# A relational graph convolution on one core: sums by chunk in place of sums by four chunks, evictions on VectorE, and two tiles in five chunks copied by SyncE and ScalarE

## The chip, the core and the metric

The kernel runs on one core of a Trainium2 chip. A core has five engines, each with an instruction queue of its own that it works off in order: TensorE (PE, matmuls, with its weight loads shown as PEld), VectorE (DVE), ScalarE (ACT), GpSimd (POOL) and SyncE (SP, which here only issues DMAs). Engines wait for each other, and for DMAs, by semaphores. The metric is the device time of one execution in microseconds; smaller is better.

## The reference

Two layers of a relational graph convolution on 50,000 nodes of 128 features, 850,000 edges of which 50,000 are loops (the last of each node's run), 16 relations made of 8 bases, then a residual layer norm:

```python
def _rgcn_layer(h, src, dst, rel, basis, w_comp, loop_w, bias):
    W = jnp.einsum('rb,bio->rio', w_comp, basis)
    seg = dst.astype(jnp.int32) * N_REL + rel.astype(jnp.int32)
    agg = jax.ops.segment_sum(h[src], seg, num_segments=N_ENT * N_REL)
    agg = agg.reshape(N_ENT, N_REL, -1)
    msg = jnp.einsum('nri,rio->no', agg, W)
    out = msg + h @ loop_w + bias
    return jax.nn.relu(out)
...
h = _rgcn_layer(entity_emb, src, dst, rel_type, basis1, w_comp1, loop_w1, bias1)
h = _rgcn_layer(h, src, dst, rel_type, basis2, w_comp2, loop_w2, bias2)
return h
...
x = _layernorm(x + _L0_gnn_ref(x, ...), axis=-1)
```

The edges come sorted by their destination `dst`. All is fp32.

## The kernel before

**Tiles and chunks.** A tile is 128 edges, a chunk `K` = 10 tiles. The edges that aren't loops make `C` = 625 chunks a layer, 1,250 in both. As the edges are sorted, a tile reaches few destination nodes: each tile has a window of `WN` = 12 consecutive nodes, called slots, and a chunk 120 slots. Nodes are worked on in groups of 512 (97 or 98 a layer), each held as 128 partitions of `J` = 4 nodes.

**A chunk's way through the engines.**

- GpSimd fetches the source rows of every tile by one indirect DMA of 128 rows of 512 B (`gather`, line 202). `rows` is a ring of `GATHERS` = 5 chunks, 50 tiles; the fetch is issued `FETCH` = 2 chunks ahead in the program, and a tile's buffer may be refilled once the product of the tile that was in it (50 tiles back) is done.
- VectorE makes, per chunk, the mask of slots `own` (line 869) and the scaled mask `hot` (line 876): for each edge, basis and slot, the edge's weight in that basis where the edge belongs to that slot. The weights come from one-hot relations (`weights`, load at line 617, comparison at 624, matmuls into `fixed` at 629), once for four chunks.
- TensorE multiplies a tile's rows by its part of `hot` (line 974): 128 features by 8 bases x 12 slots. Five such products fill one PSUM bank (`pa`, two banks).
- ScalarE copies five products at a time into `aT` (line 982). `aT` holds four chunks (`BATCH` = 4), 480 slots for each basis.
- Once in four chunks `slots_of_batch` sums over the bases: eight matmuls of 480 columns with the basis as stationary operand (line 746), spread over the following tiles; ScalarE copies the result, which has the slots along its columns, into `by_slot` (line 752); TensorE turns it back with four transposes (line 756); VectorE spreads each slot's row to its place among the `J` nodes of a partition (`spread_out`, line 734, tile `slots`).
- `LAG` = 6 chunks later `to_nodes` adds the slots to the node groups in PSUM (line 788, tile `pn`, with the mask of line 771), and the loop term with `loop_w` (line 798).
- Beside that, `from_itself` works out per group of 512 nodes what the loop edges give: load `h_own` (line 677, SyncE), transposes (687), a copy to `hT` by ScalarE (691), 16 matmuls into `po` (702, two banks), each scaled by VectorE into `by` (709), and a reduction by VectorE (717). `loop_weights` gives the scales (load at 644, comparison 655, matmuls 662, copy 670).
- `finish` adds both parts (809), and does the relu (812, ScalarE) and the store to `H` (813, SyncE) in layer 0, or the residual and the layer norm (`normed`, 576 to 587) and the store to the output (818) in layer 1.

**Order.** TensorE, GpSimd, VectorE and ScalarE run in the order in which the program is written (`manual_schedule`); the function `beside` places the side work at fixed tiles of a chunk: a step of `from_itself` at tiles 0, 5 and 7, a step of the batch's sums at tiles 1, 3, 6 and 9, a step of `finish` at 2, 6 and 9, the node sums at 8. SyncE issues its loads and stores in program order too. The last five chunks of a layer are summed one by one, in `slots` (line 724): eight matmuls of 128 columns with a basis of `aT` as the stationary operand, whose result needs no transpose. An fp32 matmul shows as two records in the trace, a transpose as one.

**Set-up.** At the beginning and beside the first chunks, `runs` removes the loops from runs of 672 edges and `rows_of` puts the remaining edges' sources, slots and relations into tables (`src`, `key`, `REL`), a block of 128 rows of 640 edges at a time.

Of the kernel before, what the change touches and what calls it, by code (L numbers as in the profile page):

```python
# [40 lines left out]
I32 = mybir.dt.int32  # L41
# [31 lines left out]
BATCH = 4  # L73
LAG = BATCH + 2
# [8 lines left out]
def tile_rgcn_resnorm(  # L83
# [33 lines left out]
    assert D == P and N >= P and edges.shape[0] == 1 and AT * NR == P and PER * NB * WN <= BANK and AT * PER * NB == WEIGHTS and PER == HALF and S <= P and C >= 4 and M > 0 and N % C == 0 and N % J == 0 and J * D == BANK and C % BATCH == 1 and C > 4 * BATCH and RUN - LK // 2 == LIVE and 2 * C <= NG * P and N <= 1 << 16 and E % ROW == 0  # L117
# [9 lines left out]
    REL = dram.tile([2 * C, LIVE], U8, name="REL")  # L127
    NL = -(-(N + LK) // GN) * GN
# [309 lines left out]
    def rows_of(j, pool):  # L438
# [35 lines left out]

        begin = pool.tile([P, HALF], F32, name="begin")
# [113 lines left out]
    def chunked():  # L589
        with (  # L590
# [7 lines left out]

            ALONE = C - BATCH - 1

# [12 lines left out]
            def weights(c, n):  # L613
# [9 lines left out]
                is_rel = hp.tile([P, LIVE], F32, name="is_rel", bufs=1)  # L623
# [14 lines left out]
            def loop_weights(g, n):  # L638
# [14 lines left out]
                is_rel = rel.bitcast(F32)  # L653
                for h in range(2):
                    nc.vector.tensor_scalar(is_rel[:m, h, :], rel[:m, h, :], its_rel1[:m], None, op0=OP.is_equal)
                    if h == 0:
                        yield
                po = ps_o.tile([P, BANK], F32, name="po")
                of = po[:, : J * T * NB].rearrange("p (j t) -> p j t", j=J)
                for j in range(J):  # L660
                    for h in range(2):
                        nc.tensor.matmul(  # L662
                            of[:, j, :],
                            is_rel[:m, h, :].rearrange("k (p j) -> k p j", j=J)[:, :, j],
                            EACH[n][:m, :T, :].rearrange("k t b -> k (t b)"),
                            start=h == 0,
                            stop=h == 1,
                        )
# [4 lines left out]
            def from_itself(g, of, n):  # L673

                m = nodes(g)
                h = sb.tile([P, J, D], F32, name="h_own", bufs=1)
# [43 lines left out]
            def slots(c, k, aT, n):  # L720
# [7 lines left out]
                yield spread_out(c, ps[:, :D])  # L728

            def spread_out(c, of):  # L730

                k = ks(c) * WN
                st = sb.tile([P, J, D], F32, name="slots", bufs=BATCH)
                nc.vector.tensor_tensor(  # L734
                    st[:k],
                    of[:k, None, :].to_broadcast([k, J, D]),
                    which[:k, c, :, None].to_broadcast([k, J, D]),
                    op=OP.mult,
                )
                return st  # L740

            def slots_of_batch(c, aT, st, n):

                ps = ps_s.tile([P, BANK], F32, name="ps")
                for b in range(NB):
                    nc.tensor.matmul(  # L746
                        ps[:, : BATCH * S], BASIS[n][:, b, :], aT[:, b, :], start=b == 0, stop=b == NB - 1
                    )
                    if b < NB - 1:
                        yield  # L750
                by_slot = sb.tile([P, BATCH * S], F32, name="by_slot", bufs=1)
                nc.scalar.copy(by_slot, ps[:, : BATCH * S])  # L752
                yield
                po = ps_o.tile([P, BANK], F32, name="po")
                for q in range(BATCH):
                    nc.tensor.transpose(po[:S, q * P : (q + 1) * P], by_slot[:, q * S : (q + 1) * S], ident)  # L756
                    if q == 1:
                        yield
                for q in range(BATCH):
                    st[c + q] = spread_out(c + q, po[:, q * P : (q + 1) * P])  # L760
                    if q == 1:
                        yield
                yield
# [60 lines left out]

            loaded, stored = [0], [1]
# [36 lines left out]
            for n, of in enumerate((x, H1)):  # L862
# [21 lines left out]
                def sum_up(c):  # L884
                    at = c % BATCH * S
                    for st[c] in slots(c, ks(c), aTs[c // BATCH][:, :, at : at + S], n):
                        yield

                def added_in(c):

                    if c < ALONE + 2:
                        return [c - LAG] if c >= LAG else []
                    at = ALONE - BATCH + 2 * (c - ALONE - 2)
                    return [at, at + 1] if c < C else list(range(at, C))

                def own_of_all():

                    for g in range(NGR):
                        while now[0] < min(first(g) + LAG - 5, C - LAG - 2):
# [9 lines left out]
                def add(c):  # L909

                    for g in to_nodes(c, n):
                        assert made[0] > g
                        ending.append(finish(g, n))

                def beside(t, c, owning, summing):
# [3 lines left out]
                    if c < ALONE + 2:  # L919
                        if t in (1, 3, 6, 9):  # L920
                            next(summing, None)
                    elif 1 <= t <= 4:
                        for _ in range(NB // 4):
                            next(summing, None)
                        if t == 4:
                            done(summing)
                            if c == C - 1:
                                done(sum_up(c - 1))
# [3 lines left out]
                    if t == 8:  # L932
                        for one in added_in(c):
                            add(one)
# [3 lines left out]
                now, made = [0], [0]  # L938
                owning = own_of_all()
                for c in range(C):  # L940
                    now[0] = c
                    if n == 0 and c:

                        next(coming, None)
                        while ready[0] + 1 < len(ROWS) and 2 * min(C, c + FETCH + 5) > ROWS[ready[0] + 1]:
                            next(coming)
                    for to in range(0 if c == 0 else c + FETCH, min(C, c + FETCH + 1)):
                        buffer = (n * C + to) % GATHERS
                        for k in range(ks(to)):
                            gather(rows[buffer][:, k, :], of, src[:, to * K + k : to * K + k + 1])  # L950
                    g = rows[(n * C + c) % GATHERS]
# [7 lines left out]
                    if c % BATCH == 0:  # L959
                        aTs[c // BATCH] = hp.tile([P, NB, BATCH * S], F32, name="aT")  # L960
                    aT, place_of = aTs[c // BATCH], c % BATCH * S
                    if c >= ALONE + 2:
                        if c == ALONE + 2:
                            done(summing)
                        summing = sum_up(c - 2)
                    elif c % BATCH == 0:
                        summing = slots_of_batch(c - BATCH, aTs[c // BATCH - 1], st, n) if c else iter(())
                    for k in range(0, K, PER):
# [3 lines left out]
                        for i in range(PER):  # L972
                            if i < m:
                                nc.tensor.matmul(  # L974
                                    pa[:, i * NB * WN : (i + 1) * NB * WN],
                                    g[:, k + i, :],
# [4 lines left out]
                            if i == m - 1:  # L981
                                nc.scalar.copy(  # L982
                                    aT[:, :, place_of + k * WN : place_of + (k + m) * WN].rearrange(
                                        "d b (i w) -> d i b w", w=WN
                                    ),
                                    pa[:, : m * NB * WN].rearrange("d (i b w) -> d i b w", i=m, w=WN),
                                )
                            beside(k + i, c, owning, summing)
                    if c + 2 < C:
# [6 lines left out]
                    for one in added_in(c + 1) if c + 1 < C else ():  # L996
                        masks[one] = masks_of(one)
# [6 lines left out]
                for one in added_in(C):  # L1004
                    masks[one] = masks_of(one)
                    if one == C - 1:
                        done(sum_up(one))
                    add(one)
# [193 lines left out]
```

## Time and profile before

| | |
|---|---|
| three runs | 18,435.78, 18,461.99, 18,465.47 us |
| median | 18,461.99 us |
| profiled execution | 18,435.78 us, its span 18,434.0 us |
| mean granted TensorE clock | 0.762 |
| instruction records | 136,664 |
| 12,500 gathers (line 202), two groups | 5,929.8 + 5,938.3 us busy |
| products (line 974) | 25,000 records, 4,581.9 us busy |
| sums of four chunks (746) and transposes (756) | 4,960 and 1,240 records, 2,910.5 and 317.9 us busy |
| sums of one chunk (724) | 160 records of 277 ns |
| node sums (788) | 4,128 records, 2,553.4 us busy |
| loop edges (702) | 3,136 records, 2,048.6 us busy |
| software DMA queue (the gathers) | 403,552 packets, 17.1% of 16 engines |
| hardware DMA queue (SyncE) | 132,551 packets, 3.5% |

How to read it: the page's first line gives for each engine its busy time, that as a share of the span, and the number of its records. A group's line has line, engine, operation, the tile written and those read, the shape and the count; behind the bar the busy time, the mean duration of one in ns, and behind the second bar the engine's idle time ahead of these instructions with what ended most of it. In the list of waits a line reads: engine, tile and line that waited, what it waited for, the us in total, the times, the longest. "issue" is time in which an engine waited for nothing that the profile shows, "remote" a wait whose releaser isn't known. Ends of matmuls are modelled.

### The profile page before, as it was taken

To read this page: it belongs to the slowest core of one execution; us is meant where nothing else is said; L and a number is where in the kernel's file an instruction comes from. 1 tells how busy PE (TensorE), PEld (TensorE's weight loads), DVE (VectorE), ACT (ScalarE), POOL (GpSimd) and SP (SyncE) were. 2 spreads that over 40 slices of the span, in tenths; PEclk is the share of its full clock that TensorE was granted. 3 is DMA by queue.
4 is the path that set the end of the run, shared out by engine and by line. 5 is a ranking of instruction groups with operands and counts; after the bars stand their busy time and mean duration, and the time that the engine had idled before them with its cause. 6 is when DMAs were issued, how large, how long until landed. Compare 5 with 4: busy or idle time off the path is not lost. (4 is left out here: it accounts for less than half of the span.)

```text
span 18434.0 us, 136664 instructions
## 1 busy us (share of the span) xinstructions
PE 11416.0 (62%) x45072; PEld 7482.7 (41%) x45072; DVE 6704.1 (36%) x11496; ACT 1926.2 (10%) x3706; POOL 11894.1 (65%) x12533
## 2 busy tenths in 40 slices
PE   4565555656566666666656666666666666666666
PEld 3343333434344444444444444444444444444444
DVE  4344344444333333333333333333333333333333
ACT  0010000101000000010101111111111111111111
POOL 5666666666666666666656666666666666666665
PEclk8777777777777777777777777777777777777777
DMA  2222222222122122221212222222222222222221
GB/s 70 62 60 58 56 58 60 61 59 60 53 54 55 54 54 54 54 54 54 55 49 57 57 57 57 57 57 57 57 57 58 57 57 57 57 57 57 57 57 51
DMA packets 540034, 1044.31 MB, mean 57 GB/s; under 512 B 214689, under 2 KB 259011, under 8 KB 539319
## 3 DMA queue, kind: packets, MB, share of 16 engines
q0 software_dynamic: 403552, 826.82, 17.1%
q1 hardware_dynamic: 132551, 207.21, 3.5%
q8 instruction: 364, 5.96, 0.1%
q14 instruction: 351, 2.88, 0.0%
q10 hardware_dynamic: 3216, 1.45, 0.0%
HBM read 962.30 MB, written 72.31 MB: 56 GB/s over the span
## 5 line engine op out<-in xcount | busy, mean ns | idle before, releaser
L202 POOL DMA_INDIRECT g<-H,src x6250 | 5929.8, 949 | 3090.0 <-issue 1304.3
L202 POOL DMA_INDIRECT g<-in_x_dram,src x6250 | 5938.3, 950 | 3029.0 <-issue 1267.5
L974 PEld LDWEIGHTS pa<-hot,g 128*128 128x128 f32 x25000 | 4547.2, 229 | 6044.9 <-issue 5010.2
L974 PE MATMUL pa<-hot,g 128*128 128x96 f32 x25000 | 4581.9, 308 | 3009.5 <-issue 2081.6
L746 PE MATMUL ps<-aT,basis 128*128 128x480 f32 x4960 | 2910.5, 672 | 707.7 <-ACT aT L982 476.2
L982 ACT COPY aT<-pa 128x480 f32<-128x480 f32 x2500 | 1388.0, 558 | 15113.3 <-remote 8194.1
L788 PE MATMUL pn<-slots,own 120*128 120x512 f32 x4128 | 2553.4, 741 | 615.4 <-DVE slots L734 289.2
L702 PE MATMUL po<-basis,hT 128*128 128x512 f32 x3136 | 2048.6, 741 | 1319.1 <-DVE by L709 1101.2
L709 DVE TENSOR_TENSOR by<-po,lw 128x512 f32<-128x512 f32 x1568 | 1069.5, 687 | 4167.5 <-remote 1469.1
L876 DVE TENSOR_TENSOR hot<-fixed,own 128x960 f32<-128x960 f32 x1250 | 1447.1, 1158 | 2091.2 <-remote 1580.7
L734 DVE TENSOR_TENSOR slots<-po,which 120x512 f32<-120x512 f32 x1240 | 782.6, 683 | 2747.6 <-remote 933.8
L717 DVE TENSOR_REDUCE ls<-by 128x128 f32<-128x1152 f32 (+1 forms) x784 | 1664.2, 2123 | 34.1
L788 PEld LDWEIGHTS pn<-slots,own 120*128 120x128 f32 x4128 | 865.5, 238 | 1202.2 <-issue 687.4
L746 PEld LDWEIGHTS ps<-aT,basis 128*128 128x128 f32 x4960 | 879.1, 221 | 754.3 <-ACT aT L982 494.9
L702 PEld LDWEIGHTS po<-basis,hT 128*128 128x128 f32 x3136 | 563.8, 225 | 1390.6 <-DVE by L709 1151.7
L869 DVE TENSOR_TENSOR own<-fixed,key 128x120 bf16<-128x120 f32 x1250 | 344.5, 276 | 2106.3 <-remote 1040.9
L756 PE MATMUL po<-ident,by_slot 128*120 128x128 f32 x1240 | 317.9, 348 | 1129.2 <-ACT by_slot L752 742.8
L756 PEld LDWEIGHTS po<-ident,by_slot 128*120 128x120 f32 x1240 | 178.3, 181 | 1171.5 <-ACT by_slot L752 770.4
L771 DVE TENSOR_SCALAR own<-col,node 120x128 f32<-120x128 f32 x2064 | 529.4, 296 | 10.4 <-PE pn L788 10.4
L629 PE MATMUL fixed<-each,is_rel 128*128 128x64 f32 x3140 | 457.2, 300 | 8.4 <-DVE is_rel L624 6.1
L629 PEld LDWEIGHTS fixed<-each,is_rel 128*128 128x128 f32 x3140 | 444.1, 221 | 9.4 <-DVE is_rel L624 7.3
L798 PEld LDWEIGHTS pn<-loop,hT 128*128 128x128 f32 x1568 | 234.5, 213 | 134.0 <-issue 133.6
(137 smaller groups left out, 2892.7 us busy)
## 6 DMA issues: line engine op xcount, KB each, us to landing
g<-in_x_dram,src POOLq DMA_INDIRECT x6250
g<-H,src POOLq DMA_INDIRECT x6250
rel<-REL SPq DMA_DIRECT2D x312, 80.0 KB
h_own<-in_x_dram SPq DMA_DIRECT2D x97, 256.0 KB
xw<-in_x_dram SPq DMA_DIRECT2D x97, 256.0 KB
H<-ls SPq DMA_DIRECT2D x97, 256.0 KB
h_own<-H SPq DMA_DIRECT2D x97, 256.0 KB
out_dram<-ls SPq DMA_DIRECT2D x97, 256.0 KB
```

Source lines behind the costliest of these rows:

```text
L202: return nc.gpsimd.indirect_dma_start(out=to, out_offset=None, in_=of, in_offset=bass.IndirectOffsetOnAxis(ap=idx, axis=0))
L629: nc.tensor.matmul(of[:, :, j * NB : (j + 1) * NB], is_rel[:m, j * P : (j + 1) * P], EACH[n][:m], start=True, stop=True,)
L702: nc.tensor.matmul(hb[:m], hT[:, j, :m], BASIS[n][:, b : b + few, :].rearrange("p b d -> p (b d)"), start=True, stop=True,)
L709: nc.vector.tensor_tensor(by[:m, b : b + few, :], hb[:m].rearrange("p (b d) -> p b d", d=D), lw[:m, j, g % T, b : b + few, None].to_broadc ...
L717: nc.vector.tensor_reduce(ls[:m, j, :], by[:m].rearrange("p b d -> p d b"), AX.X, OP.add)
L734: nc.vector.tensor_tensor(st[:k], of[:k, None, :].to_broadcast([k, J, D]), which[:k, c, :, None].to_broadcast([k, J, D]), op=OP.mult,)
L746: nc.tensor.matmul(ps[:, : BATCH * S], BASIS[n][:, b, :], aT[:, b, :], start=b == 0, stop=b == NB - 1)
L771: nc.vector.tensor_scalar(own[:k], col4[:k], node4[:k, c : c + 1], float(-g * GN), op0=OP.subtract, op1=OP.is_equal)
L788: nc.tensor.matmul(sums[g], own, of[:k].rearrange("s j d -> s (j d)"), start=c == first(g), stop=c == final(g),)
L876: nc.vector.tensor_tensor(hot[:, : ks(c)], pm[:, c % Q * K : c % Q * K + ks(c), :, None].to_broadcast([P, ks(c), NB, WN]), own[:, : ks(c), ...
L974: nc.tensor.matmul(pa[:, i * NB * WN : (i + 1) * NB * WN], g[:, k + i, :], hot[:, k + i].rearrange("e b w -> e (b w)"), start=True, stop=True,
L982: nc.scalar.copy(aT[:, :, place_of + k * WN : place_of + (k + m) * WN].rearrange("d b (i w) -> d i b w", w=WN), pa[:, : m * NB * WN].rearr ...
```

## The change

`BATCH`, `LAG`, `slots_of_batch` and `by_slot` go. Each chunk is now summed by itself in `slots`, two chunks after its products (tiles 1 to 4), VectorE spreads the sum straight from PSUM, and the node sums follow one chunk later (tile 8). `aT` holds one chunk and has three buffers; `slots` has three. The products are copied out of PSUM by VectorE instead of ScalarE. In every fifth chunk SyncE, and in another every fifth ScalarE, fetches one of the ten tiles in place of GpSimd: row by row, 128 DMAs of 512 B whose source offsets are loaded into registers from a table in DRAM (`ROW_AT`, written by `rows_of`), 32 at a time. These row DMAs are spread over the five chunks before, 45 steps of two or three rows, and begin six chunks ahead; each engine has two such tiles. That makes 248 tiles per engine, so 496 of the 12,500 gathers go, and 63,488 row DMAs come. `h_own` and `is_rel` get two buffers in place of one, the loop weights' comparison a tile of its own, and the set-up's rows are made ready five chunks earlier.

```diff
-BATCH = 4
-LAG = BATCH + 2
+SP_EVERY = 5
+ACT_EVERY = 5
+OFFSETS = 32
...
+        row_at = pool.tile([P, LIVE], F32, name="real").bitcast(I32)[:, : 2 * P]
+        nc.vector.tensor_scalar(
+            row_at[:m], srcf[:m, LIVE - 2 * P :], float(N - 1), float(4 * D), op0=OP.min, op1=OP.mult
+        )
+        nc.sync.dma_start(ROW_AT[r0 : r0 + m].rearrange("r t e -> r (t e)"), row_at[:m])
...
-                is_rel = hp.tile([P, LIVE], F32, name="is_rel", bufs=1)
+                is_rel = hp.tile([P, LIVE], F32, name="is_rel")
...
-                h = sb.tile([P, J, D], F32, name="h_own", bufs=1)
+                h = sb.tile([P, J, D], F32, name="h_own", bufs=2)
...
-                yield spread_out(c, ps[:, :D])
-
-            def spread_out(c, of):
...
-            def slots_of_batch(c, aT, st, n):
...
+                st = sb.tile([P, J, D], F32, name="slots")
                 nc.vector.tensor_tensor(
-                    st[:k],
-                    of[:k, None, :].to_broadcast([k, J, D]),
-                    which[:k, c, :, None].to_broadcast([k, J, D]),
+                    st[: k * WN],
+                    ps[: k * WN, None, :D].to_broadcast([k * WN, J, D]),
+                    which[: k * WN, c, :, None].to_broadcast([k * WN, J, D]),
                     op=OP.mult,
                 )
-                return st
+                yield st
...
+            behind = {}
+            HANDS = ((nc.sync, SP_EVERY, SP_EVERY - 1), (nc.scalar, ACT_EVERY, ACT_EVERY // 2 - 1))
+
+            def by_hand(c):
+
+                if ks(c) < K:
+                    return []
+                return [i for i, (_, every, at) in enumerate(HANDS) if c > every and c % every == at]
+
+            def row_by_row(i, c, of):
+
+                engine, every, _ = HANDS[i]
+                tile_at = 1 - by_hand(c).index(i)
+                row_at = hp.tile([1, P], I32, name=f"row_at{i}", bufs=2)
+                nc.sync.dma_start(row_at, ROW_AT[2 * c + 1 : 2 * c + 2, tile_at])
+                to = hp.tile([P, D], F32, name=f"by_hand{i}", bufs=2)
+                byte = of.bitcast(U8).rearrange("n d -> (n d)")
+                yield to
+                steps = every * (K - 1)
+                for step in range(steps):
+                    for e in range(step * P // steps, (step + 1) * P // steps):
+                        if e % OFFSETS == 0:
+                            with tc.issue_after(behind[i]) if i in behind else ExitStack():
+                                _, offsets = nc.values_load_multi_w_load_instructions(
+                                    row_at[:, e : e + OFFSETS],
+                                    engines=[engine.engine],
+                                    min_val=0,
+                                    max_val=(N - 1) * 4 * D,
+                                    skip_runtime_bounds_check_because="sources are clamped to N - 1, and none is below 0",
+                                )
+                        row = to.bitcast(U8)[e : e + 1, :]
+                        behind[i] = engine.dma_start(row, byte[None, ds(offsets[e % OFFSETS], 4 * D)]).ins
+                    yield to
...
-                    if c < ALONE + 2:
-                        if t in (1, 3, 6, 9):
-                            next(summing, None)
-                    elif 1 <= t <= 4:
+                    if 1 <= t <= 4:
                         for _ in range(NB // 4):
                             next(summing, None)
...
-                    if t == 8:
-                        for one in added_in(c):
-                            add(one)
+                    if t == 8 and c > 2:
+                        for g in to_nodes(c - 3, n):
+                            assert made[0] > g
+                            ending.append(finish(g, n))
...
-                        for k in range(ks(to)):
+                        for k in range(ks(to) - len(by_hand(to))):
                             gather(rows[buffer][:, k, :], of, src[:, to * K + k : to * K + k + 1])
-                    g = rows[(n * C + c) % GATHERS]
+                    for i, (_, every, _) in enumerate(HANDS):
+                        to = c + every + 1
+                        if to < C and i in by_hand(to):
+                            fetching[i] = row_by_row(i, to, of)
+                            handed.setdefault(to, {})[K - 1 - by_hand(to).index(i)] = next(fetching[i])
+                    g, others = rows[(n * C + c) % GATHERS], handed.pop(c, {})
...
-                    if c % BATCH == 0:
-                        aTs[c // BATCH] = hp.tile([P, NB, BATCH * S], F32, name="aT")
...
+                    aT = aTs[c] = hp.tile([P, NB, S], F32, name="aT", bufs=3)
+                    summing = sum_up(c - 2) if c > 1 else iter(())
...
-                                    g[:, k + i, :],
+                                    others.get(k + i, g[:, k + i, :]),
...
-                                nc.scalar.copy(
-                                    aT[:, :, place_of + k * WN : place_of + (k + m) * WN].rearrange(
-                                        "d b (i w) -> d i b w", w=WN
-                                    ),
+                                nc.vector.tensor_copy(
+                                    aT[:, :, k * WN : (k + m) * WN].rearrange("d b (i w) -> d i b w", w=WN),
                                     pa[:, : m * NB * WN].rearrange("d (i b w) -> d i b w", i=m, w=WN),
                                 )
                             beside(k + i, c, owning, summing)
+                            if k + i < K - 1:
+                                for each in fetching.values():
+                                    next(each, None)
```

## The prediction

> **What bounds the kernel now.** I read the busy line and the costliest groups first, then the list of waits, then single windows and the timeline. From the page:
>
> ```profile
> PE 11416.0 (62%) x45072; PEld 7482.7 (41%) x45072; DVE 6704.1 (36%) x11496; ACT 1926.2 (10%) x3706; POOL 11894.1 (65%) x12533
> L202 POOL DMA_INDIRECT g<-H,src x6250 | 5929.8, 949 | 3090.0 <-issue 1304.3
> L974 PE MATMUL pa<-hot,g 128*128 128x96 f32 x25000 | 4581.9, 308 | 3009.5 <-issue 2081.6
> L746 PE MATMUL ps<-aT,basis 128*128 128x480 f32 x4960 | 2910.5, 672 | 707.7 <-ACT aT L982 476.2
> L982 ACT COPY aT<-pa 128x480 f32<-128x480 f32 x2500 | 1388.0, 558 | 15113.3 <-remote 8194.1
> L709 DVE TENSOR_TENSOR by<-po,lw 128x512 f32<-128x512 f32 x1568 | 1069.5, 687 | 4167.5 <-remote 1469.1
> L756 PE MATMUL po<-ident,by_slot 128*120 128x128 f32 x1240 | 317.9, 348 | 1129.2 <-ACT by_slot L752 742.8
> ```
>
> No engine is full. GpSimd is the nearest: a gather is 0.95 us busy, and where the timeline shows several in a row 0.30 us of "issue" follows each, so 12,500 gathers need 12,500 x 1.25 = 15,625 us of 18,434. The other 2.8 ms are waits, and the list of waits says whose:
>
> ```profile
> PE pa L974 <- issue: 2081.6, 524, 31.3
> POOL g L202 <- remote: 1822.6, 1379, 6.1
> POOL g L202 <- PE pa L974: 1139.3, 1805, 5.8
> PE po L702 <- DVE by L709: 1101.2, 258, 28.7
> PE pa L974 <- ACT aT L982: 833.2, 135, 54.4
> PE po L756 <- ACT by_slot L752: 742.8, 120, 50.5
> PE ps L746 <- ACT aT L982: 476.2, 91, 26.8
> PE po L756 <- issue: 351.5, 106, 13.4
> PE pn L788 <- DVE slots L734: 289.2, 73, 12.6
> PE ps L746 <- issue: 224.2, 130, 14.3
> ```
>
> GpSimd waits for TensorE to release ring buffers; no wait of TensorE for a gather is among its large ones. So the ring of 50 tiles is mostly full, and TensorE's side sets the pace. What that pace is made of shows in the timeline around 12,025 us:
>
> ```profile
> 12024.42 0.58 PE L974 MATMUL pa<-hot,g 128*128 128x96 f32 x4
> 12030.83 0.56 ACT L982 COPY aT<-pa 128x480 f32<-128x480 f32 x1 [8.03 <-remote]
> 12031.90 0.68 PE L756 MATMUL po<-ident,by_slot 128*120 128x128 f32 x2 [6.91 <-ACT by_slot L752]
> ```
>
> The products end by the records at 12,025.0, yet ScalarE, idle, copies them at 12,030.8: the result counts as ready 5.8 us late (likewise the weights' products that end at 12,097.8 are used by VectorE, L869, at 12,103.4). TensorE has meanwhile run out of work whose inputs are ready and stands 6.9 us until the batch's copy is there. Two windows, without and with gathers, show the pace (columns: window, length, then busy us and count of PE, PEld, DVE, ACT, POOL; PE clock, DMA share, GB/s):
>
> ```profile
> 9352.00:9392.00 40.00, 38.42 (x224) 27.82 (x223) 22.72 (x36) 6.11 (x11) 3.51 (x5) 1.00 0.05 16
> 16000.00:16040.00 40.00, 30.79 (x117) 18.69 (x118) 25.07 (x41) 5.74 (x12) 25.77 (x28) 0.81 0.22 58
> ```
>
> 224 matmul records in 40 us at the end of layer 0, with 5 gathers; 117 with 28. The mixes differ, so I don't take the ratio as a price, but steady work costs 40/117 = 0.34 us a record.
>
> **The change part by part.** The profiled run took 18,435.8 us (span 18,434.0), 0.14% under the median 18,462; the sum is made on 18,436 and 26 us are added.
>
> *Gathers.* 248 tiles for each of SyncE and ScalarE leave the gathers: 496 x 1.25 = 620 us less on GpSimd. It counts only where GpSimd is the limit; 2.8 ms of its time are waits already. Between 0 and -620 I take -300.
>
> *Batches.* 310 copies (L752), 1,240 transposes and the wide sums with their waits go: 742.8 + 351.5 + 476.2 + 224.2 = 1,795 us of TensorE standing on lines that vanish. The new sums read a tile evicted over a chunk earlier, and the node sums read slots about 1.4 chunks old, 20 us at 14.7 us a chunk, beyond the some 6 us that results are late. If TensorE merely waits elsewhere, half remains: -900 to -1,795; I take -1,795, because the cover of 20 us is large.
>
> *TensorE.* Out go 4,960 records (2,910 us busy) and 1,240 transposes (318 us); in come 19,840 narrow records (10,000 matmuls of two records, 160 of which exist already in the last chunks as L724, 277 ns each): 19,840 x 0.277 = 5,496 us. Net +2,268 us, 13,640 records more (+30%). Low end 0, if the narrow ones overlap as well as the wide; high end 13,640 x 0.34 = +4.6 ms by the window. I take +2,268, the nearest row.
>
> The Trainium skill, in "TensorE: Matmul & The Clock Gate", section "Wait — 56ns, not 53.3ns?", says that back-to-back matmuls start N columns apart at the array's clock. By columns nothing changes: 16 records x 480 + 4 x 128 = 8,192 a batch before, 64 x 128 = 8,192 after. By that rule this term is nought and the total 17.5 ms. The 277 ns of L724 are durations, not start to start, so I don't follow it.
>
> *Eviction on VectorE.* 2,500 x 0.687 (L709's row, the nearest read of one PSUM bank) = +1,718 us, against 0.558 on ScalarE, which was idle in front of nearly each. VectorE goes from 36% to some 46%, in order: an eviction stands behind a reduction of 2.12 us (L717) or a mask of 1.16 us (L876). TensorE has two product banks and refills one every 18,434/2,500 = 7.4 us, while the product counts as ready some 6 us late; what the eviction adds is thus hardly hidden. Low end 0; high end 46% of a mean remainder of 0.9 us plus 0.13 us longer = 0.55 us x 2,500 = +1,370. I take half, +700. Behind it wait the scalings L709, which free `po` for TensorE: the 1,101 + 289 us that TensorE waits for VectorE grow with its load, 46/36, by about +300 (0 to 700).
>
> *Semaphores.* TensorE gets some 1,700 more wait instructions, as a tile copied by hand waits for up to eight semaphores. Bounds 0 and 0.24 us each (the idle "issue" that the timeline shows between weight loads): +100.
>
> *Row copies.* 496 x 128 = 63,488 DMAs of 512 B, half on each queue. A single-row DMA (L287) occupies SP 0.25 to 0.29 us, so 31,744 x 0.27 = 8.6 ms a queue, hidden. But the instruction list gives all DMAs of both queues eight semaphores in turn, each waiting for the one eight before, so at most eight fly. How long a row flies no row shows. The nearest are larger loads at the start:
>
> ```profile
> 0.76 0.40 SPq L281 DMA_DIRECT2D d_i<-in_edges_dram  x1
> 3.77 0.15 DVE L331 CAST run_first<-d_i 128x1 f32<-128x1 int32 x1 [1.29 <-DMA d_i<-in_edges_dram]
> ```
>
> 3.0 us from issue to use for 336 KB; L644's 128 KB take 2.6 us. One 512 B row: between 1.2 (four issues) and 2.6 us; with eight in flight 9.5 to 20.6 ms. I take 2.2 us: 17.5 ms, just hidden, cost 0. What queues behind: ScalarE's copies of `hT` (L691) and its relu and norm, SP's loads of `h_own`, `rel` and the stores; and as the semaphores are shared, an SP store waiting for ScalarE (L813 waited 870 us before) holds ScalarE's rows too.
>
> The Trainium skill puts the fixed cost of one DMA at about 2.0 us ("DMA: Bandwidth & Descriptors", section "Anatomy of one DMA — SWDGE (gpsimd) path"), which would give an estimated 15.9 ms here; its section "Issuing engines are not separate DMA queues" says that several issuers save issue time only, a rule that speaks against spreading such copies over two engines. No run here shows either for rows yet.
>
> *Loads.* The second buffers of `h_own` and `is_rel` take SP's waits apart; these sit off TensorE's path (TensorE stood 35 us in all before the transposes of `h_own`): 0.
>
> Sum: 18,436 - 300 - 1,795 + 2,268 + 700 + 300 + 100 = 19,709; + 26 = about **19,740 us**. Own range 18,700 to 21,400 (the narrow records and the batch waits carry it).
>
> **Rivals.** *TensorE's records don't bind* (faster): narrow sums overlap, term 0, VectorE's eviction mostly hidden (+400): 18,462 - 300 - 1,795 + 400 + 300 + 100 = about 17,170. For it: PE is busy 62% only, and the first window above passes 224 records in 40 us. Against it: results already arrive 6 us late when gathers run, and a record of 480 columns takes 672 ns, 2.4 times that of 128, not 3.75 times.
>
> *The row copies bind* (slower): it decides once a row flies longer than 2.4 us: 63,488 / 8 x 2.4 = 19.0 ms, and 5% more where a waiting store stands in the turn (L813 and L818 waited 1.6 ms for ScalarE, 9% of the span; half of it), 20.0 ms. At 2.6 us: 20.6 ms bare, 21.7 with it; I price it between, at 21,100. Then TensorE waits at its `by_hand` products and the gathers stop behind it. For it: the 2.6 and 3.0 us rows, and the coupled queues; against: rows are small.
>
> *No net change*: the batch waits pay exactly for the records and evictions: 18,462.
>
> **How the numbers follow.** Main case 0.50, row copies bind 0.23, records don't bind 0.22, no net change 0.05. The time is the main case's, 19,740. The range reaches from 17,600 (most of the faster case lies below) to 22,600 (row copies at 2.7 us with the 5%), with some 0.2 left out. A measurement tells 0.2%, 37 us, from no change: faster 0.22, same 0.04, slower 0.74.
>
> **What would show it.** Main case: PE busy above 13 ms, `by_slot` waits gone, new PE waits on VectorE `aT`, GpSimd waiting for PE still. Records don't bind: narrow sums' group near 2.9 ms busy, GpSimd's "issue" the largest wait. Row copies bind: large PE waits on DMA `by_hand`, rows spaced 0.3 us on SP and ScalarE nearly throughout. I am wrong if GpSimd's waits for PE fall under 1 ms in all.

## The result, and the profile after

The changed kernel takes 22,285.6 us (four runs, 22,265 to 22,300) where the kernel before takes 18,461.5 on the same chip: 1.207 times as long, 95% interval 1.205 to 1.210. It is 3.82 ms slower; 1.28 ms slower had been forecast.

The engine line and the groups that answer to those shown of before, from the page of the changed kernel:

```profile
PE 12149.2 (55%) x58712; PEld 9182.9 (41%) x58712; DVE 8268.7 (37%) x14006; ACT 421.1 (2%) x896; POOL 11429.7 (51%) x12037
L972 PE MATMUL pa<-hot,g 128*128 128x96 f32 x24008 | 4840.8, 311 | 2467.4 <-issue 1524.7
L980 DVE COPY aT<-pa 128x480 f32<-128x480 f32 x2500 | 1633.3, 653 | 7334.7 <-remote 3354.2
L710 PE MATMUL po<-basis,hT 128*128 128x512 f32 x3136 | 2108.3, 760 | 3905.3 <-ACT hT L699 2911.9
L732 PE MATMUL ps<-basis,aT 128*120 128x128 f32 x20000 | 3844.4, 318 | 631.9 <-issue 570.4
```

TensorE has 13,640 records more, yet only 12,149.2 - 11,416.0 = 733 us more of busy time; of the 3,829 us by which the span grew, 3,096 are idle time. The granted clock fell from 0.762 to 0.725; busy time, where that would show, grew by those 733 us only. The narrow sums take 3,844 us where the wide ones and their transposes took 2,910 + 318. So look at what TensorE waits for. From the list of waits of the changed kernel (engine, tile and line, what it waits for, us in all, times, longest):

```profile
POOL g L204 <- PE pa L972: 5307.8, 1890, 31.0
PE po L710 <- ACT hT L699: 2911.9, 155, 68.0
DVE is_rel L630 <- DMA rel<-REL: 1812.9, 112, 68.7
PE pa L972 <- issue: 1554.2, 969, 38.2
PE po L670 <- DVE is_l L661: 1036.7, 80, 49.3
PE pa L972 <- DVE aT L980: 712.9, 248, 49.6
PE po L695 <- DMA h_own<-H: 544.5, 29, 29.4
PE pn L768 <- DVE own L751: 537.5, 74, 53.4
PE po L710 <- DVE by L717: 435.0, 136, 26.4
PE po L695 <- DMA h_own<-in_x_dram: 168.0, 8, 29.8
```

The waits of the batch (742.8 + 351.5 + 476.2 + 224.2) are gone. New are waits for things that come late out of the two queues with row copies: `hT`, which ScalarE copies (2,912 us), the comparison of the loop weights, whose table SyncE loads (1,037), `h_own`, which SyncE loads (544.5 + 168.0), and a mask (538) that stands on VectorE behind `is_rel`, for which SyncE loads `rel`. That is 5.2 ms, where the same waits of before came to 0.2. GpSimd waits for TensorE 5.3 ms in place of 1.1.

The timelines of the two queues near 16,000 us show the reason. First SyncE, then ScalarE with TensorE (start, length, what, how many):

```profile
15999.00 9.09 SPq L836 DMA_DIRECT2D by_hand<-H  x18
16008.15 0.63 SPq L623 DMA_DIRECT2D rel<-REL  x1
```

```profile
16000.24 7.68 ACTq L836 DMA_DIRECT2D by_hand<-H  x22
16008.01 0.58 ACT L699 COPY hT<-po 128x512 f32<-128x512 f32 x1 [64.21 <-DMA by_hand<-H]
16008.24 16.04 ACTq L836 DMA_DIRECT2D by_hand<-H  x31
16008.65 2.08 PE L710 MATMUL po<-basis,hT 128*128 128x512 f32 x2 [16.86 <-ACT hT L699]
16010.58 0.55 DVE L630 TENSOR_SCALAR is_rel<-rel,its_rel 128x640 f32<-128x640 uint8 x1 [18.21 <-DMA rel<-REL]
```

Both queues issue row after row, 0.35 to 0.52 us each, and the copy of `hT` and the load of `rel` come when the rows ahead of them are out. TensorE has stood 16.9 us by then, VectorE 18.2. SyncE itself hardly waits for anything but DMAs: its largest two waits are for the flights of earlier rows, 847 and 773 us.

### The profile page after: what moved, and what is told of

Same layout as the page of the kernel before. It is cut to its first block, busy times and chain, and to the rows that moved or that the text cites. A ratio compares the mean times of both kernels' runs of the same rounds, so it can differ in the third digit from the quotient of the medians.

```text
span 22263.4 us, 293484 instructions
## 1 busy us (share of the span) xinstructions
PE 12149.2 (55%) x58712; PEld 9182.9 (41%) x58712; DVE 8268.7 (37%) x14006; ACT 421.1 (2%) x896; POOL 11429.7 (51%) x12037
## 5 line engine op out<-in xcount | busy, mean ns | idle before, releaser
L204 POOL DMA_INDIRECT g<-H,src x6002 | 5700.8, 950 | 5180.6 <-PE pa L972 2736.4
L204 POOL DMA_INDIRECT g<-in_x_dram,src x6002 | 5703.0, 950 | 5004.7 <-PE pa L972 2571.4
L972 PE MATMUL pa<-hot,g 128*128 128x96 f32 x24008 | 4840.8, 311 | 2467.4 <-issue 1524.7
L980 DVE COPY aT<-pa 128x480 f32<-128x480 f32 x2500 | 1633.3, 653 | 7334.7 <-remote 3354.2
L732 PE MATMUL ps<-basis,aT 128*120 128x128 f32 x20000 | 3844.4, 318 | 631.9 <-issue 570.4
L732 PEld LDWEIGHTS ps<-basis,aT 128*120 128x120 f32 x20000 | 3127.3, 218 | 727.5 <-issue 652.3
L737 DVE TENSOR_TENSOR slots<-ps,which 120x512 f32<-120x512 f32 x1250 | 856.1, 685 | 692.9 <-PE pa L972 331.6
L670 PE MATMUL po<-each,is_l 64*128 64x32 f32 (+1 forms) x800 | 205.1, 419 | 1074.7 <-DVE is_l L661 1036.7
L670 PEld LDWEIGHTS po<-each,is_l 64*128 64x128 f32 (+1 forms) x800 | 193.2, 324 | 1089.9 <-DVE is_l L661 1049.9
L695 PE MATMUL po<-ident,h_own 128*128 128x128 f32 (+1 forms) x784 | 205.1, 350 | 743.2 <-DMA h_own<-H 544.5
```

The costliest lines, as they stand in the source:

```text
L204: return nc.gpsimd.indirect_dma_start(out=to, out_offset=None, in_=of, in_offset=bass.IndirectOffsetOnAxis(ap=idx, axis=0))
L732: nc.tensor.matmul(ps[: k * WN, :D], aT[:, b, : k * WN], BASIS[n][:, b, :], start=b == 0, stop=b == NB - 1)
L737: nc.vector.tensor_tensor(st[: k * WN], ps[: k * WN, None, :D].to_broadcast([k * WN, J, D]), which[: k * WN, c, :, None].to_broadcast([k * ...
L972: nc.tensor.matmul(pa[:, i * NB * WN : (i + 1) * NB * WN], others.get(k + i, g[:, k + i, :]), hot[:, k + i].rearrange("e b w -> e (b w)"), ...
L980: nc.vector.tensor_copy(aT[:, :, k * WN : (k + m) * WN].rearrange("d b (i w) -> d i b w", w=WN), pa[:, : m * NB * WN].rearrange("d (i b w) ...
```

## The experiments

Three theories stand against each other. P is the forecast's main case: 30% more TensorE records, results that count as ready late, and evictions on VectorE. R says that the loss lies in the row copies, by R1, the eight semaphores that the two queues share, or by R2, what stands behind rows on its own queue. Q and C are later forms of it: Q, a queue binds when its own serial work doesn't fit into five chunks; C, the queues hold each other up through the shared semaphores. That the two queues share eight shows in the changed kernel's trace: every row, load and store of both tells its landing by one of the same eight semaphores, each used 8,125 or 8,126 times.

One thing came in between: not every chip gives the same times. On most the kernel before takes 15.80 to 15.82 ms, on the chip of the result, and on those of the last five runs below, 18.45 to 18.46. So each time stands beside the kernel before on its own chip.

**The kernels unchanged, on a 15.8 ms chip.**

> The kernel before, unchanged, for a profile on the chip of these runs. The first four experiments ran on a chip on which it takes 15.80 ms, not 18.46. Theory L (on the first chip TensorE's results count as ready late, here not): at 15.8 ms GpSimd is the bound, 12,500 gathers x 1.25 us = 15.6 ms, GpSimd's waits for TensorE are below 0.3 ms and ScalarE's product copies start within 1 us of the products' ends. At 18.4 ms: waits as in the profile before.

> The changed kernel, unchanged, beside the others on one chip. R (its loss lies in the row copies' queues, whatever the chip): where before takes 15.8 ms it takes 19 to 21.5 ms, with TensorE's waits for hT near 3 ms. P (its loss lies in TensorE's late results): where before takes 15.8 ms it takes 15.5 to 16.5 ms.

Before: 15,806.2 us. Changed: 17,454.8, ratio 1.104 (1.102 to 1.106), 1.65 ms slower. GpSimd's and TensorE's waits of the kernel before on this chip:

```profile
POOL g L202 <- PE pa L974: 656.3, 2154, 0.3
PE pa L974 <- DMA g<-H,src: 1529.1, 2230, 5.0
PE pa L974 <- DMA g<-in_x_dram,src: 1500.0, 2070, 24.8
PE po L756 <- ACT by_slot L752: 26.4, 89, 0.7
```

Here TensorE waits for gathers, 3.0 ms, and GpSimd for TensorE never more than 0.3 us: that is the spacing which a gather costs in any case. The kernel is bound by 12,500 x 1.25 = 15.6 ms of gathers. What TensorE and its late results cost the kernel before on the chip of the result is absent here, and yet the changed kernel loses 1.65 ms: P, which gave it at most 16.5 ms, isn't the whole. R's 19 ms was too much as well. The changed kernel's TensorE waits here are the same as above, hT first:

```profile
PE po L710 <- ACT hT L699: 3091.4, 187, 43.0
PE po L670 <- DVE is_l L661: 1086.7, 92, 39.6
PE po L695 <- DMA h_own<-H: 644.1, 31, 31.7
```

**Without row copies.**

```diff
-                if ks(c) < K:
+                if ks(c) <= K:
                     return []
```

> The changed kernel without its row copies: all 12,500 tiles are gathered, the sums by chunk and VectorE's evictions stay. Theory R (the row copies hold up what stands behind them on SyncE and ScalarE): TensorE's waits for hT (2,912 us), for the loop weights' comparison (1,037) and for h_own (712) go, 4.7 ms of 22.3, and up to 0.6 ms of gathers come back: 17.6 to 18.4 ms. Rival P (30% more TensorE records and the evictions set the pace, as the forecast had it): 19.7 to 22 ms.

15,798.3 us, ratio 0.9997 (0.9987 to 1.0006); in four more runs on 15.8 ms chips 0.9999, 1.0001, 0.9999 and 0.9998. Sums by chunk and evictions on VectorE cost nothing that can be measured there, and the whole 1.65 ms is the row copies'. The time is under R's range because that was worked out for a chip of 18.46 ms. The repeats were meant for such a chip and did not meet one:

> The changed kernel without row copies a third time, for a chip on which before takes 18.46 ms as in the result. R (there too the row copies make the whole loss: SyncE's row instructions take up to 1.4 us each there, on the 15.8 ms chips 29 ns and 0.23 us): 17.6 to 18.8 ms. P (30% more TensorE records with late results, VectorE's evictions): 19.7 to 22 ms. Where before takes 15.8 ms: 15.80 again, which tells nothing new.

**And with the evictions on ScalarE again.**

```diff
-                                nc.vector.tensor_copy(
+                                nc.scalar.copy(
```

> The same with the 2,500 evictions back on ScalarE: only the sums by chunk differ from before. Where before takes 18.46 ms: the evictions' term of the forecast was 700 us, so by P 0.5 to 1 ms less than without row copies; by R within 0.3 ms of it. Where before takes 15.8 ms: 15.80.

15,822.1 us, ratio 0.9999 (0.9989 to 1.0009). With either engine's evictions GpSimd is the bound on these chips.

**One hand only: SyncE, then ScalarE.**

```diff
-            HANDS = ((nc.sync, SP_EVERY, SP_EVERY - 1), (nc.scalar, ACT_EVERY, ACT_EVERY // 2 - 1))
+            HANDS = ((nc.sync, SP_EVERY, SP_EVERY - 1),)
...
+            HANDS = ((nc.scalar, ACT_EVERY, ACT_EVERY // 2 - 1),)
```

> Only SyncE copies a tile by hand in every fifth chunk, ScalarE none. Theory R with the eight shared semaphores as the limit (R1): half the rows, so at least 31,744 / 8 x 2.2 us = 8.7 ms, far from binding: within 2% of the kernel without row copies. R2 (each queue's own work behind its rows): SyncE's loads of rel, lrel and h_own are still late, worth up to 1.8 + 0.7 ms of waits: 19 to 20.5 ms. P: no change against the kernel without rows.

> Only ScalarE copies a tile by hand in every fifth chunk, SyncE none. R1: within 2% of the kernel without row copies. R2: ScalarE's copies of hT still stand behind rows, so the 2.9 ms for which TensorE waits for hT stay in part: 19.5 to 21.5 ms. P: no change against the kernel without rows.

SyncE alone: 15,489.1 us, ratio 0.980 (0.979 to 0.982), which is 248 x 1.25 = 310 us for the gathers saved and nothing lost. R1 said so, R2 not: SyncE's loads do stand behind rows, but early enough, as TensorE waits 119 us for the loop weights' comparison and 99 for `h_own`. ScalarE alone: 18,175.7 us, 1.150 (1.148 to 1.152), slower than both hands together: R1 had it within 2%, and R2's range, 19.5 to 21.5 ms, was worked out for a chip of 18.46 ms. The timeline of ScalarE, then that of SyncE, in this run:

```profile
12012.87 0.59 ACT L699 COPY hT<-po 128x512 f32<-128x512 f32 x1 [40.88 <-DMA by_hand<-H]
12015.19 31.59 ACTq L836 DMA_DIRECT2D by_hand<-H  x56
12046.82 0.30 ACT L587 ACTIVATE sd<-mv,eps 128x4 f32<-128x4 f32 x1 [33.36 <-DMA by_hand<-H]
```

```profile
12030.89 0.35 SPq L767 DMA_DIRECT2D xw<-in_x_dram  x1
```

56 rows take 31.6 us, though the 32 rows before `hT` had taken 10.6. The single records have a hole from 12,023.1 to 12,033.6: the next row's semaphore had its turn with SyncE's load of `xw`, which was issued at 12,030.9 only. SyncE in turn stood for turns that ScalarE's rows held (it waited 1.8 and 1.5 ms for `by_hand` DMAs of the two layers ahead of its loads of offsets alone). Summed over this trace, ScalarE's rows wait 4.5 ms for SyncE's loads of `rel`, `h_own`, `xw` and `lrel`. Meanwhile `hT` and the norm wait behind the rows, TensorE for `hT` 5.5 ms in all. With SyncE's loads and ScalarE's rows in one ring of eight, each stands for the other: this is C, and R1's count of flights alone missed it.

**Every tenth chunk, both hands; and SyncE alone every tenth.**

```diff
-SP_EVERY = 5
-ACT_EVERY = 5
+SP_EVERY = 10
+ACT_EVERY = 10
```

The second run has, besides, the `HANDS` of SyncE alone.

> Both queues copy, but a tile in every tenth chunk each: 31,744 rows over both queues. R1 (semaphores shared by both queues): 8.7 ms of lane time, not binding, about 18.5 ms, like one queue alone. R2: half the load on each queue, so half of the loss, 19.5 to 20.5 ms. P: about 22 ms less nothing, no change against the changed kernel beyond 2%.

> The changed kernel with one hand only: SyncE copies a tile in every tenth chunk, 15,872 rows in place of 63,488, 124 gathers fewer. Where before takes 18.46 ms, SyncE's row instructions came 0.59 us apart at the worst, 15,872 x 0.59 = 9.4 ms, which fits: R 17.4 to 18.6 ms, P 19.5 to 22 ms. Where before takes 15.8 ms, GpSimd is the bound: 124 x 1.25 = 155 us less, 15.65 ms.

15,497.1 us, 0.981 (0.979 to 0.982), and 15,648.8 us, 0.990 (0.989 to 0.992): once more 1.25 us for each gather saved (248 and 124) and no loss. Half the rows over both queues cost nothing; R2's half a loss isn't there (the expected times were again those of an 18.46 ms chip). With both hands the loss comes all at once, between half and full load, which speaks for a queue that is full; ScalarE alone, which lost 15% with half of the rows, shows that the number of rows isn't all.

**`hT` off ScalarE.**

```diff
-                nc.scalar.copy(hT[:, :, :m], po.rearrange("p (j e) -> p j e", j=J)[:, :, :m])
+                nc.vector.tensor_copy(hT[:, :, :m], po.rearrange("p (j e) -> p j e", j=J)[:, :, :m])
...
-                nc.scalar.copy(lw, of.rearrange("p j (t b) -> p j t b", b=NB))
+                nc.vector.tensor_copy(lw, of.rearrange("p j (t b) -> p j t b", b=NB))
```

> The changed kernel with the 196 copies of hT and the 50 of the loop weights on VectorE, so that TensorE waits for nothing behind ScalarE's rows but the ends of the node groups. R2 (copies stand behind rows on ScalarE): TensorE's wait for hT goes, 1.5 to 3 ms faster than the changed kernel. R1 (both queues' rows and loads share eight semaphores, so the queues crawl in step): less than 0.7 ms faster, since the loads of rel, lrel and h_own stay late. P: no faster, VectorE has 0.13 ms more to do.

17,476.3 us, 1.106 (1.104 to 1.108), no better than 17,454.8, as R1 and P had it and R2 not, though the largest wait falls from 3,091 to 890 us. The list of waits tells where it went:

```profile
DVE is_rel L630 <- DMA rel<-REL: 2523.9, 151, 49.2
PE po L670 <- DVE is_l L661: 1155.9, 95, 38.0
PE po L710 <- DVE by L717: 1003.4, 114, 49.8
PE po L710 <- DVE hT L699: 889.6, 72, 43.8
PE pa L972 <- DMA by_hand<-in_x_dram: 814.0, 83, 23.3
```

Against the changed kernel on this chip, `is_rel` waits 0.8 ms more for SyncE's load (1,696 us there), the loop edges' products 0.7 ms more for VectorE (331 there), and the products of layer 0 0.6 ms more for rows copied by hand (242 there). The late `hT` was a symptom; whichever copy or load is next on a full queue takes its place.

**How full the queues are.** For the changed kernel on the 15.8 ms chip: SyncE's timeline over about one tile, and the offset loads (count, then shortest, median and longest in ns):

```profile
11999.94 2.17 SPq L836 DMA_DIRECT2D by_hand<-H  x7
12002.16 0.64 SPq L623 DMA_DIRECT2D rel<-REL  x1
12002.91 14.39 SPq L836 DMA_DIRECT2D by_hand<-H  x26
12017.40 0.22 SPq L819 DMA_DIRECT2D row_at<-ROW_AT  x1
12017.72 15.07 SPq L836 DMA_DIRECT2D by_hand<-H  x33
12032.97 0.38 SPq L798 DMA_DIRECT2D out_dram<-ls  x1
12033.45 19.92 SPq L836 DMA_DIRECT2D by_hand<-H  x44
```

```profile
L828 SPq TENSOR_LOAD <-row_at x992: 2030/2127/4383, 52.8 to 17416.4; - x199
SPq L836 <- DMA by_hand<-in_x_dram: 1597.3, 2870, 9.2
SPq L836 <- DMA by_hand<-H: 1515.5, 2982, 7.5
```

There is no gap here in which SyncE has nothing to do. A tile costs it 128 rows at 2.17 / 7 = 0.31 us, 40 us; four offset loads of 2.13, 8.5; waits for semaphores held by rows, (1,597.3 + 1,515.5) / 248 = 12.6: 61 us, and its other loads and stores. Five chunks with 48 gathers left last 48 x 1.25 = 60 us. It doesn't fit, and the kernel takes 17,455 / 250 = 69.8 us for five chunks. With SyncE alone the same waits are next to nothing (for the second layer none is listed):

```profile
SPq L836 <- DMA by_hand<-in_x_dram: 4.5, 9, 0.9
```

Added up over the whole trace, a queue's time is its instructions, the waits that a DMA ended, the waits that another engine ended, and pauses ahead of an instruction in which no wait shows (us):

| queue, run | span | instructions | pauses | waits for DMAs | waits for engines |
|---|---|---|---|---|---|
| SyncE, changed kernel, 15.8 ms chip | 17,454 | 11,047 | 2,151 | 4,092 | 139 |
| SyncE, SyncE alone | 15,489 | 11,289 | 2,451 | 137 | 1,579 |
| ScalarE, ScalarE alone | 18,150 | 10,750 | 2,354 | 4,859 | 171 |
| SyncE, changed kernel, chip of the result | 22,263 | 12,799 | 7,571 | 1,744 | 137 |
| SyncE, SyncE alone every fourth chunk | 23,416 | 15,388 | 7,536 | 369 | 93 |

A queue that waits for other engines has room; that of SyncE alone has 1.6 ms of it. In the other rows hardly any is left: the queue sets the pace (with ScalarE alone in part at second hand, as some of SyncE's loads that it waits for stood for VectorE or TensorE themselves). On the 15.8 ms chips SyncE's own instructions and pauses, 53 us a tile, would fit into the 60, so Q in its first form doesn't explain the loss there; the 17 us of waits for DMAs push it over. With the same rows on SyncE and none on ScalarE these waits are 0.6 us a tile, so they come from the second queue, as C says: of those ahead of SyncE's rows, two thirds (2.3 of 3.4 ms) are for rows that ScalarE issued. On the chip of the result the own instructions and pauses alone, 82 us a tile, are more than the 74 that the kernel before takes for five chunks.

**The rest of the runs** met chips of the 18.46 ms kind, so that what they were to show on the others stays untried, and expected times that were made for 15.8 ms don't apply. ScalarE every tenth chunk, SyncE every fifth:

```diff
-ACT_EVERY = 5
+ACT_EVERY = 10
```

> SyncE copies a tile in every fifth chunk, ScalarE in every tenth. In the changed kernel's trace on a 15.8 ms chip SyncE and ScalarE issue rows 0.325 us apart and stand 2.1 to 2.2 us at each of a tile's four offset loads: 128 x 0.325 + 4 x 2.2 = 50 us a tile. Theory Q (a queue binds when its own work doesn't fit): ScalarE 50 of 124 us, SyncE 50 of 62: both fit, 372 gathers less are worth 372 x 1.25 = 465 us, 15.3 to 15.5 ms where before takes 15.8. Theory C (rows of one queue wait on the shared semaphores for DMAs that the other can't issue yet): 16 to 17.5 ms.

22,762.7 us, 1.233 (1.231 to 1.235). ScalarE's rows were halved, and it is no faster than the changed kernel (1.207): there SyncE's queue alone is enough to hold up everything. In this run's trace it is left with less than 0.1 ms of waits for other engines. SyncE alone, every fourth chunk:

```diff
-SP_EVERY = 5
+SP_EVERY = 4
...
+            HANDS = ((nc.sync, SP_EVERY, SP_EVERY - 1),)
```

> SyncE alone, a tile in every fourth chunk. Q: 310 tiles x 50 us = 15.6 ms and 0.6 ms of SyncE's other DMAs do not fit into 15.4 ms: 16.2 to 16.8 ms where before takes 15.8, though SyncE alone in every fifth gave 15.49. If only flights in the eight semaphores count (39,700 / 8 x 1.4 = 7 ms): 15.4 ms.

23,443.8 us, 1.270 (1.268 to 1.272), 23,444 / 310 = 75.6 us a tile on one queue, with no other queue's rows in its way. The table's last row shows it: 22.9 of 23.4 ms are the queue's own instructions and pauses. One load of offsets a tile (the rows of a tile then repeat every 32):

```diff
-                        if e % OFFSETS == 0:
+                        if e == 0:
```

> The changed kernel with one load of 32 offsets a tile in place of four; the rows of a tile then repeat every 32, so the sums are those of other edges; all DMAs stay. Q: 3 x 2.2 us less for each of 248 tiles on each queue, 1.6 ms less of serial work, 15.7 to 16.3 ms where the changed kernel takes 17.45. C or the number in flight: less than 0.5 ms faster.

> The changed kernel with one offset load a tile in place of four, again; where before takes 18.46 ms it took 20.97, 1.3 ms less than the changed kernel. Q on a 15.8 ms chip: the changed kernel takes 17.45 there; 3 x 2.2 us x 248 = 1.6 ms less work on each queue brings 15.7 to 16.3 ms. If the number in flight or the order of copies behind rows made the loss: above 17 ms.

20,967.3 us, 1.135 (1.133 to 1.137), and 20,930.1 in the second run, 1.134 (1.132 to 1.136): 1.32 and 1.36 ms less than the changed kernel, with every DMA still there. Off each queue went 3 x 2.1 us x 248 = 1.6 ms of its own work (by the traces 1.4 on SyncE and 1.6 on ScalarE), and most of that came out of the time. That is Q on a chip like that of the result. ScalarE alone with more buffers for SyncE's loads:

```diff
-                h = sb.tile([P, J, D], F32, name="h_own", bufs=2)
+                h = sb.tile([P, J, D], F32, name="h_own", bufs=3)
...
-                rel = hp.tile([P, LIVE], U8, name="rel")
+                rel = hp.tile([P, LIVE], U8, name="rel", bufs=4)
...
-                rel = hp.tile([P // 2, 2, GN], I32, name="lrel", bufs=1)
+                rel = hp.tile([P // 2, 2, GN], I32, name="lrel", bufs=2)
...
-                            xw = xws[g] = sb.tile([P, J, D], F32, name="xw", bufs=2)
+                            xw = xws[g] = sb.tile([P, J, D], F32, name="xw", bufs=3)
...
-            HANDS = ((nc.sync, SP_EVERY, SP_EVERY - 1), (nc.scalar, ACT_EVERY, ACT_EVERY // 2 - 1))
+            HANDS = ((nc.scalar, ACT_EVERY, ACT_EVERY // 2 - 1),)
```

> Only ScalarE copies, as in the run that took 18.18 ms, with more buffers for what SyncE loads (h_own and xw 3 in place of 2, rel 4 in place of 2, the loop weights 2 in place of 1), so that SyncE need not hold a semaphore's turn while it waits for a buffer. C: ScalarE's rows stood 4.4 ms for SyncE's loads there; most of it goes, 15.6 to 16.8 ms. Q: ScalarE's own work is the same, 18.0 to 18.3 ms.

24,104.0 us, 1.306 (1.304 to 1.308). The time is inconclusive, as the kernel without these buffers was not run on such a chip. In the trace ScalarE's rows wait 2.0 ms for the four loads, not 4.5, but ScalarE's pauses are 10.3 ms in place of 2.4. That ScalarE alone costs more than both hands holds there too.

## Why the prediction was wrong

The direction was right and the time inside the range, but the size was a third of the real one, and the likeliest case was the wrong one. That the range held it is luck: it reached so far for rows that fly 2.7 us, which they don't.

- *Row copies, cost 0.* This is the step that failed: "31,744 x 0.27 = 8.6 ms a queue, hidden" and "I take 2.2 us: 17.5 ms, just hidden, cost 0". The first counted the DMA instruction alone. A row also has a register move, and starts 0.31 to 0.33 us after the last; a tile has four offset loads of 2.1 us, 2.1 ms a queue, which stand in the diff and which I never priced. With the waits for semaphores it is 61 us a tile on the 15.8 ms chips, 15.1 ms before SyncE's own loads and stores. On the chip of the result SyncE's queue has 20.4 ms of instructions and pauses and 1.7 of waits for DMAs where I had put 8.6, hidden. The flight was off the other way: on the 15.8 ms chip a row's landing shows 1.6 us after its issue (median; four in five lie between 1.2 and 1.9), so eight in flight would need 63,488 / 8 x 1.6 = 12.7 ms, not 17.5. The 2.0 us that I cited are, by that section's title, of DMAs issued by GpSimd; these rows come from SyncE and ScalarE. I had two limits, issue and flight, both under the span, and treated them as alternatives; on a queue that works in order, waits come on top of issue.
- *What queues behind: 0.* Named correctly (`hT`, `rel`, `h_own`), and it is there that the loss shows, 5 ms of new TensorE waits. A full queue has no early loads. The same holds for *Loads, 0*: `h_own` came late, 0.7 ms.
- *The rival "row copies bind"* had the right part, at 0.23 and 21.1 ms, but for another reason, a row's flight beyond 2.4 us. Of its marks, the rows close upon each other on both queues came, the large waits for them did not: TensorE waits for the `by_hand` tiles themselves by hardly 0.2 ms in the changed kernel. A tile fetched by hand begins six chunks ahead; what stands behind its rows has less slack.
- *TensorE's records, +2,268 us.* Mis-sized: busy time rose by 3,844 - 2,910 - 318 = 616 us, 192 ns a narrow record in place of 277. I took a duration for a start-to-start time; the same row of L724 has 22.7 us of busy time for its 160 records, 142 ns each, as they overlap. The Trainium skill's rule on columns ("TensorE: Matmul & The Clock Gate", "Wait — 56ns, not 53.3ns?"), which would have given nought, was nearer than the duration I chose.
- *Evictions, +700, and +300 for what waits behind.* VectorE's 1,633 us came as priced (1,718), but TensorE's waits for the eviction are 713 us where they were 833, and for `by` 435 where they were 1,101. As the kernel now waits for its row copies, these waits don't price the term on that chip; on the 15.8 ms chips it is nought.
- *Batches, -1,795.* The waits did go.
- *Gathers, -300.* On the 15.8 ms chips each gather saved is worth its whole 1.25 us (310 us for 248). On the chip of the result nothing of it shows, as GpSimd waits for TensorE 4.2 ms longer.
- *Semaphores, +100.* No run here prices it.

Open is what the sums by chunk and the evictions do alone on a chip of 18.46 ms: the run without row copies met none. The terms above, as the trace has them, would make the kernel faster there rather than slower; that is argued, not shown. How much of the 3.82 ms is the row copies' is thus known on the 15.8 ms chips only, where it is all of 1.65; for the chip of the result it is shown that their queues are full.

## What to carry to other kernels

Price a DMA stream by everything that its queue executes, register moves and offset loads too, and add the waits between its DMAs: on a queue that works in order these add up, and once the sum passes the time that other engines leave, everything else on that queue comes late. Two issuing queues that take turns on the same semaphores are not independent; half of the rows, spread over both or all on SyncE, made the kernel 2% faster here on the 15.8 ms chips, while the same half on ScalarE alone cost 15% and the full set on both 10%. If removing the largest wait changes nothing, look for what made its releaser late.

## What the runs showed of the hardware

The same kernel differs by 17% between chips, 15.80 and 18.46 ms, each within 0.2% of itself. On the slower kind TensorE's results count as ready some 6 us after the records end, as shown of before; on the other ScalarE's copy follows at once:

```profile
12024.27 0.36 PE L974 MATMUL pa<-hot,g 128*128 128x96 f32 x2
12024.67 0.56 ACT L982 COPY aT<-pa 128x480 f32<-128x480 f32 x1 [6.79 <-PE pa L974]
```

The instructions of the issuing queues differ too, those that only move a register for one. In the changed kernel SyncE's row instructions (shortest, median, longest in ns), on the chip of the result:

```profile
L836 SPq MOVE by_hand<-in_x_dram x15872: 2/29/1409, 55.7 to 11357.6; - x199
```

and on a 15.8 ms chip:

```profile
L836 SPq MOVE by_hand<-in_x_dram x15872: 29/29/42, 55.2 to 8793.7; - x199
```

The pauses of SyncE's queue are 7.6 ms there and 2.2 here. The DMA queues moved the same packets. The granted clock of the kernel before is lower there, 0.762 against 0.831, but on a 15.8 ms chip the run of ScalarE alone shows 0.766 with no such pauses. What delays moves and results on one kind of chip no run here tells. With it the whole change cost 3.8 ms, without it 1.65.
